# A graph layer on one core: eight of nine one-hot tiles of a part's sums move from VectorE to GpSimd, between the gathers

## The chip, the core and the metric

The kernel runs on one core of one Trainium2 chip. A core has five engines that run side by side and meet at semaphores: TensorE (PE in the profile; PEld is its weight load), VectorE (DVE), ScalarE (ACT), GpSimd (POOL) and SyncE (SP), which only issues DMAs here. The metric is the device time of one execution in microseconds; smaller is better.

## The reference

A graph of 12,500 nodes with 128 features and 412,500 edges, sorted by destination, goes through one gated message-passing layer, a residual and a layer norm:

```python
theta = x[dst] - x[src]
w = sigmoid(relu(theta @ W1 + b1) @ W2 + b2)
agg = segment_sum(w * theta, dst, num_segments=n_nodes)
indeg = segment_sum(ones((E, 1)), dst, num_segments=n_nodes)
y = x + agg + indeg * (x @ W4 + b4)
out = (y - mean(y)) / sqrt(var(y) + 1e-5)        # over the 128 features
```

All of it is float32. The edge list is an input, so what is gathered and summed where is known only at run time.

## The kernel before

**Parts.** The sorted edges are cut into parts, each with a window of at most 112 destination rows. A table `z` in HBM holds `x @ W1` and `x` side by side, so that one gathered row of 256 floats serves the gate and the message. The first 26 parts (`PLAIN`) are handled in a simple way while the table and lookup tiles are being made. The other 234, the *later parts*, are the bulk of the time and the place of the change. Two successive parts make a block with one window.

**A later part.** It has two kinds of source. Eight tiles of 128 edges are gathered from `z`, one indirect DMA of GpSimd each (L380). Their slots come in pairs that share a destination, so four one-hot tiles `ow` (128 edges x 112 window rows) serve all eight. Another five tiles of 128 edges (`HQ`) come from *hot* lookups: ScalarE writes one-hot tiles `of` (L966, L968), TensorE multiplies them with resident tables (L980), ScalarE moves the result to `xT` (L994). They have five one-hot tiles `owh` of their own. The nine tiles `ow` and `owh` are "the one-hot tiles of the sums": TensorE multiplies them with the weighed messages and adds up into the PSUM tile `pa` (L1083, in `add_part`).

**The order of work.** For later parts the instructions of TensorE, VectorE and ScalarE run in the order in which `part(s)` writes them:

- VectorE: `logits` (L896, L898, L899), the five hot logits (L1054), the weighing of four gathered tiles (L928) with a gate that ScalarE makes (L903), then `owh` (L1066) and `ow` (L873). Then comes the end of the block before: in the first part of a pair `finish` (L1129, which waits for ScalarE's `total`, L1121), in the second `normalize` (L1156, L1162 and on). Last come some steps of `place`, which sorts the edges of the next 64 parts (L549, L552, L641 to L643 and others).
- ScalarE: tiles `of`, the gate (L903), hot weights (L1057, L1063), the weighing of the other four tiles (L919), `total` and so on.
- TensorE: `add_part(s - 1)`, hot products, then `products_ahead(s + 1, s + 2)` (L1021, L1025, L1029, L1040).

Both one-hots are written as one comparison each, of a row of column numbers (`iota_f`, a copy in PSUM) with each edge's row in the window (`rel` and `hrel`, bf16, one value to a partition and tile): 4 x 112 and 5 x 112 elements. `ow` has 4 buffers, `owh` 2.

**GpSimd's queue.** It holds gathers and, between every two of them, a filler: a no-operation in the first eight parts, later a memset of 128 x 320 floats that nobody reads (`rest_t`, L374). `part(s)` issues the gathers of part s+3 (`LEAD`). The first of the eight waits for the newest matmul that was issued when it was written (`paced`). There are six tiles `zbuf` for the gathered rows, used in a ring. GpSimd takes its operands from SBUF only; `iota_row` is the SBUF form of the row of column numbers.

Of the kernel before, what the change touches and what calls it, by code (L numbers as in the profile page):

```python
# [9 lines left out]
F32 = mybir.dt.float32  # L10
# [5 lines left out]
OP = mybir.AluOpType  # L16
# [4 lines left out]
P = 128  # L21
D = 128
K = 8
J = K // 2
# [3 lines left out]
WB = 112  # L28
# [10 lines left out]
LEAD = 3  # L39
LB = 5  # L40
NH = 8
# [11 lines left out]
HQ = HK // P  # L53
# [27 lines left out]
def gnn_resnorm(  # L81
# [37 lines left out]
    nc = tc.nc  # L119
# [36 lines left out]
    def set_of(s):  # L156

        s0 = 0 if s < PLAIN else PLAIN + (s - PLAIN) // S2 * S2
        return placed[s0], s - s0
# [42 lines left out]
    def early(n, dtype=F32):  # L202

        a = used_of[0]
        used_of[0] = a + -(-n // (2 if dtype == BF16 else 1))
        assert used_of[0] <= HR * HT * D
        t = tabs_flat[:, a:used_of[0]]
        return t if dtype == F32 else t.bitcast(dtype)
# [37 lines left out]
    iota_row = const.tile([P, P], F32, name="iota_row")  # L246
# [9 lines left out]
    rest = early(D)  # L256
# [7 lines left out]
    for i, t in enumerate(terms):  # L264
        at = slice(i * HALF // 2, i * HALF // 2 + 1)
# [9 lines left out]
    iota_f = fix[:, :WB].rearrange("p (o m) -> p o m", o=1)  # L275
# [60 lines left out]
    def pairs(s):  # L336
        return J if s < NF else JT

    def slots(s):
        return [h * J + j for h in range(2) for j in range(pairs(s))]  # L340
# [11 lines left out]
    def rows_of(s):  # L352
        return own_of(s)[:, :, :D] if s < NH else ring(s)[:, :, :2 * D]
# [11 lines left out]
    rest_t = const.tile([P, 320], F32, name="rest_t")  # L365
    table_steps = []
    paced = {}

    def gather(s):

        (src_i, _, _), i = set_of(s)
        for k in slots(s):
            if gathers:
                rest = nc.gpsimd.memset(rest_t, 0.0) if s >= NH else nc.gpsimd.engine_nop()  # L374
                tc.add_manual_dep(
                    rest.ins, gathers[-1].ins.name,
                    mybir.DependencyInfo(mybir.DependencyClass.NoSync, mybir.DependencyReason.DATA),
                    reason="between two gathers")
                gathers.append(rest)
            ins = nc.gpsimd.indirect_dma_start(  # L380
                out=rows_of(s)[:, k, :], out_offset=None, in_=z if s >= NH else x,
                in_offset=IndirectOffsetOnAxis(ap=src_i[:, k, i:i + 1], axis=0))
            waits = [(gathers[-1], mybir.DependencyClass.NoSync)] if gathers else []
            at = (s * K + k) * 4 * len(chunks) // (NH * K) - 6
            if s < NH and 0 <= at < len(table_steps):
                waits.append((table_steps[at], mybir.DependencyClass.Sync))
            if k == 0 and s in paced:
                waits.append((paced[s], mybir.DependencyClass.Sync))
            for other, kind in waits:
                tc.add_manual_dep(  # L390
                    ins.ins, other.ins.name,
                    mybir.DependencyInfo(kind, mybir.DependencyReason.DATA), reason="gathers' pace")
            gathers.append(ins)


    base_b = const.tile([1, NK], I32, name="base_b")
# [280 lines left out]
    with tc.manual_schedule(engines={SP}), tc.tile_pool(name="work", bufs=2) as wp, tc.tile_pool(  # L677
        name="ps_y", bufs=2, space=bass.MemoryType.PSUM
    ) as ps_y, tc.tile_pool(
        name="ps_l", bufs=1, space=bass.MemoryType.PSUM  # L680
    ) as ps_l:
        parts, blocks = {}, {}
# [18 lines left out]
        def bank(name="pxa"):  # L701
            return ps_l.tile([P, P * G], F32, name=name)
# [77 lines left out]
        def load_u(b):  # L780

            u = blocks[b]["u"] = wp.tile([P, D], F32, name="u", bufs=3)
            nc.sync.dma_start(u[:WB], u_d[ds(blocks[b]["base"], WB), :])
# [62 lines left out]
        def spread_y(s):  # L846
# [17 lines left out]
                                            y_of(s), start=s >= NH, stop=True, skip_group_check=s < NH)  # L864
            return last

        def one_hot_w(s):

            (_, rel, _), i = set_of(s)
            parts[s]["ow"] = []  # L870
            for k0 in range(0, K if s < PLAIN else J, J):
                ow = wp.tile([P, J, WB], F32, name="ow", bufs=4)
                nc.vector.tensor_tensor(  # L873
                    ow, iota_f.to_broadcast([P, J, WB]),
                    rel[:, k0:k0 + J, i:i + 1].to_broadcast([P, J, WB]), op=OP.is_equal)
                parts[s]["ow"].append(ow)
# [24 lines left out]
        def open_gate(s):  # L901

            nc.scalar.activation(gate[:, s % 2], parts[s]["lg"][:, :, 0], AF.Sigmoid, bias=b2_c)  # L903
# [26 lines left out]
        def weigh_rest(s):  # L930
            scale_rows(s, range(KV, K))

        def hot_set(s):

            s0 = PLAIN + (s - PLAIN) // S2 * S2
            return hots[s0], s - s0
# [11 lines left out]
        def hot_load(f):  # L948

            i0, g, i1, i = f  # L950
            a = i0
            while a < i1:
                (hot_s, _, n), j = hot_set(a)
                m = min(i1 - a, n - j)
                nc.sync.dma_start(
                    hot_src[:, i % NU, (a - i0) * EP:(a - i0 + m) * EP],
                    hot_s[g, j:j + m].rearrange("(o p) l e -> o (p l e)", o=1).to_broadcast([P, m * EP]))
                a += m
# [48 lines left out]
        def hot_x(s, q):  # L1007
            return parts[s]["hx"][:, q * P:(q + 1) * P] if q < G else parts[s]["hz"][:, P:2 * P]
# [50 lines left out]
        def hot_weights(s):  # L1059

            wx = parts[s]["wxh"]
            for q in range(HQ):
                nc.scalar.activation(wx[:, q, :D], hot_x(s, q), AF.Copy, scale=wx[:, q, D:D + 1])  # L1063
            (_, hrel, _), j = hot_set(s)
            owh = parts[s]["owh"] = wp.tile([P, HQ, WB], F32, name="owh")
            nc.vector.tensor_tensor(  # L1066
                owh, iota_f.to_broadcast([P, HQ, WB]),
                hrel[:, j, :].rearrange("p (q o) -> p q o", o=1).to_broadcast([P, HQ, WB]), op=OP.is_equal)

        def shift(b):  # L1070

# [51 lines left out]
        def finish(b):  # L1123

            d = blocks[b]
            a = d["a"]
            plain = b * SUB < PLAIN
            if not plain:
                nc.vector.tensor_add(a[:WB], a[:WB], d["pa"][:, 0, :])  # L1129
# [55 lines left out]
        def fetch(b):  # L1185
            if b < NK:
                load_block(b)
# [66 lines left out]
        def due_at(s, lead):  # L1254
            return [f for f in rest_of if f[0] - lead == s]
# [87 lines left out]
        def part(s):  # L1343

            b, h = divmod(s, SUB)
            credit[0] = min(credit[0] + (2.15 if s < PLAIN + S2 else 1.9), 6.0)
            if s in turns:
                edges[s + 3] = turns[s], load(turns[s])
            if s in edges:
                i, loaded = edges.pop(s)  # L1350
                assert steps[0] is None
                steps[:] = place(i, lambda: bank("last"), *loaded), "k"
            for f in rest_of:
                if f[0] - 5 == s:
                    hot_load(f)
            if h == 0:
                fetch(b + 2)
                if b - 1 in blocks and "u" not in blocks[b - 1]:
                    load_u(b - 1)
            ended = PLAIN // SUB <= b - 1 < NK  # L1360
            if opened:
                hot_out(*opened.pop())
            now = due_at(s, 3)
            if now:
                hot_tiles(now[0])
            if h == 1 and s + 3 < NS:
                one_hot(s + 3)
            if s < NS:
                logits(s)
            if PLAIN + AHEAD <= s + LEAD < NS:  # L1370
                if s >= PLAIN + 4:
                    paced[s + LEAD] = newest[0]
                gather(s + LEAD)
            if PLAIN <= s - 1 < NS:
                add_part(s - 1)
            if now:
                opened.append((now[0], hot_products(now[0])))
            if s < NS:
                open_gate(s)
                hot_logits(s)  # L1380
                weigh(s)
                hot_weights(s)
                gate_sums(s)
                one_hot_w(s)
                if now[1:]:
                    hot_out(*opened.pop())
                    hot_tiles(now[1])
                weigh_rest(s)
                advance("p")
                products_ahead(s + 1, s + 2)  # L1390
                if now[1:]:
                    opened.append((now[1], hot_products(now[1])))
            if h == 0 and ended:
                total(b - 1)
                finish(b - 1)
                own(b - 1)
            if h == 1:
                if s < NS:
                    shift(b)
                if ended:  # L1400
                    normalize(b - 1)
            spend("ksnmz")
# [7 lines left out]
    with tc.tile_pool(name="post_ps", bufs=1, space=bass.MemoryType.PSUM) as pps:  # L1410
        one = const.tile([P, 1], F32, name="one")
# [195 lines left out]
```

## Time and profile before

| | |
|---|---|
| Times of three runs | 3405.97, 3414.64, 3415.90 us (median 3414.64) |
| The profiled execution | 3395.38 us, span 3393.6 us |
| Granted TensorE clock, mean | 0.885 |
| Busy: PE, PEld | 2713.4, 2351.2 us |
| Busy: DVE, ACT, POOL | 2641.6, 2363.5, 2821.6 us |
| Later parts, in time | from about 413 us to the end |

Lines of the profile name the engine, the source line, the operation, output<-inputs and a count; "idle before" is the time that the engine stood still just ahead of the instruction, and after the arrow stands what ended it. "issue" means that nothing the profile shows was being waited for; "remote" is a source that the profile can't name. The engines' busy times overlap, so none of them is the time of the kernel, and the end of a matmul is modelled.

### The profile page before, as it was taken

The numbers are of one execution on the slowest core, as the hardware profiler recorded it, in microseconds if no ns is written. First come the engines' busy times: TensorE is split into PE (matmuls) and PEld (weight loads), VectorE is DVE, ScalarE is ACT, GpSimd is POOL, SyncE is SP. The second block draws the span as 40 slices with busy tenths as digits, with TensorE's granted clock in tenths as the row PEclk, the third lists the DMA queues.
The fourth block names the chain that finished last, engine by engine and source line by source line (L and its number), as shares of the span: only waits on it lengthen the run. The fifth ranks groups of instructions, "written<-read, shape, count | busy, mean of one in ns | idle before, by whom it ended". The sixth has DMA issues, their size and how long they took to land.

```text
span 3393.6 us, 62355 instructions
## 1 busy us (share of the span) xinstructions
PE 2713.4 (80%) x18615; PEld 2351.2 (69%) x18615; DVE 2641.6 (78%) x6197; ACT 2363.5 (70%) x5856; POOL 2821.6 (83%) x4093
## 2 busy tenths in 40 slices
PE   6776778787788787888788878888878888888887
PEld 5676767676677676777677766676667777677776
DVE  6797458898888689888888858888887866666666
ACT  4554567776677677777777767777767777777774
POOL 5678778888888888888888888888888888888883
PEclk9876678898899888999898889899988999998998
DMA  7564434444444444444444444444444444444441
GB/s 255 184 169 121 119 93 121 118 111 117 121 113 120 128 113 116 121 117 121 122 118 120 116 118 123 117 117 124 116 115 123 115 122 117 119 122 118 126 110 55
DMA packets 265060, 416.67 MB, mean 123 GB/s; under 512 B 66608, under 2 KB 178217, under 8 KB 264205
## 3 DMA queue, kind: packets, MB, share of 16 engines
q0 software_dynamic: 98528, 267.78, 28.5%
q1 hardware_dynamic: 164219, 138.42, 15.6%
q10 hardware_dynamic: 1970, 6.40, 0.5%
q8 instruction: 154, 2.52, 0.3%
q14 instruction: 189, 1.55, 0.2%
HBM read 384.89 MB, written 27.49 MB: 122 GB/s over the span
## 4 chain that ended last, share of the span: by engine, by line
DVE 30%; ACT 25%; PE 16%; issue 11%; POOL 8%; DMA 5%; another core or an unknown queue 4%; DVEq 0%; SPq 0%; POOLq 0%; ACTq 0%
POOL zbuf L380 6%; ACT wxh L1063 5%; PE pd L980 4%; DVE hh L1054 4%; DVE zbuf L896 4%; DVE zbuf L898 4%; ACT zbuf L919 4%; DVE lg L899 4%; ACT of L966 4%; PE pa L1083 4%; POOL rest_t L374 2%; DMA zbuf<-z,src_i 2%; ACT of L968 2%; DVE ed L549 2%
## 5 line engine op out<-in xcount | busy, mean ns | idle before, releaser
L380 POOL DMA_INDIRECT zbuf<-z,src_i x1866 | 1816.1, 973 | 421.0 <-issue 261.6
L980 PE MATMUL pd<-of,tabs 128*128 128x128 f32 (+4 forms) x4816 | 685.9, 298 | 181.6 <-ACT of L968 95.8
L374 POOL MEMSET rest_t<- 128x320 f32 x2010 | 800.4, 398 | 1.0
L980 PEld LDWEIGHTS pd<-of,tabs 128*128 128x128 f32 x4816 | 628.9, 209 | 224.7 <-ACT of L968 113.5
L1083 PE MATMUL pa<-zbuf,ow 128*112 128x260 f32 (+1 forms) x2282 | 588.1, 406 | 47.6 <-ACT zbuf L919 21.6
L1083 PEld LDWEIGHTS pa<-zbuf,ow 128*112 128x112 f32 x2282 | 407.4, 200 | 157.7 <-ACT zbuf L919 30.1
L1025 PE MATMUL pxa<-wni,xT 128*128 128x128 f32 x1872 | 303.8, 311 | 258.0 <-DVE hh L1054 241.5
L1025 PEld LDWEIGHTS pxa<-wni,xT 128*128 128x128 f32 x1872 | 266.1, 218 | 281.8 <-DVE hh L1054 261.0
L966 ACT ACTIVATE of<-hot_src,nodes 128x512 f32<-128x512 f16 (+3 forms) x602 | 394.1, 709 | 7.1 <-issue 4.3
L919 ACT ACTIVATE zbuf<-zbuf 128x128 f32<-128x128 f32 x1144 | 362.8, 389 | 0.4
L1040 PE MATMUL y<-y,oh 64*128 64x128 f32 x1872 | 341.1, 323 | 14.2 <-issue 14.0
L1029 PE MATMUL pxa<-y,oh 64*128 64x128 f32 x1872 | 336.9, 323 | 9.9 <-issue 9.6
L1054 DVE SCALAR_TENSOR_TENSOR hh<-pxa,w_r 128x128 f32<-128x128 f32 x936 | 270.7, 289 | 92.9 <-remote 48.2
L1083 PEld LDWEIGHTS pa<-wxh,owh 128*112 128x112 f32 x2340 | 295.2, 177 | 34.8 <-issue 12.6
L968 ACT ACTIVATE of<-of 128x1024 f32<-128x1024 f32 (+3 forms) x301 | 310.8, 1033 | 9.2
L1083 PE MATMUL pa<-wxh,owh 128*112 128x130 f32 x2340 | 308.9, 276 | 5.8 <-issue 4.4
L994 ACT ACTIVATE xT<-pd 128x512 f32<-128x512 f32 (+7 forms) x496 | 185.7, 416 | 183.2 <-PE pd L980 59.5
L1029 PEld LDWEIGHTS pxa<-y,oh 64*128 64x128 f32 x1872 | 275.2, 219 | 49.5 <-issue 26.9
L928 DVE TENSOR_TENSOR zbuf<-zbuf,fix 128x512 f32<-128x512 f32 x234 | 160.2, 684 | 186.4 <-ACT fix L903 118.9
L896 DVE TENSOR_TENSOR zbuf<-y,zbuf 128x1024 f32<-128x1024 f32 x234 | 285.5, 1220 | 13.5 <-issue 3.5
L898 DVE SCALAR_TENSOR_TENSOR zbuf<-zbuf,fix 128x1024 f32<-128x1024 f32 x234 | 285.7, 1221 | 8.0
L899 DVE TENSOR_REDUCE lg<-zbuf 128x8 f32<-128x1024 f32 x234 | 285.5, 1220 | 8.0
(265 smaller groups left out, 4710.0 us busy)
## 6 DMA issues: line engine op xcount, KB each, us to landing
to_all<-off_d SPq DMA_DIRECT2D x234, 144.0 KB
hot_src<-hot_s SPq DMA_DIRECT2D x257, 128.0 KB
zbuf<-z,src_i POOLq DMA_INDIRECT x1866
z<-zbuf SPq DMA_DIRECT2D x8, 1024.0 KB
xw<-in_x_dram SPq DMA_DIRECT2D x130, 56.0 KB
u<-u_d SPq DMA_DIRECT2D x130, 56.0 KB
out_dram<-o SPq DMA_DIRECT2D x130, 56.0 KB
y<-z SPq DMA_DIRECT2D x252, 28.0 KB
```

The lines of the kernel that those rows point to most:

```text
L374: rest = nc.gpsimd.memset(rest_t, 0.0) if s >= NH else nc.gpsimd.engine_nop()
L380: ins = nc.gpsimd.indirect_dma_start(out=rows_of(s)[:, k, :], out_offset=None, in_=z if s >= NH else x, in_offset=IndirectOffsetOnAxis(ap= ...
L896: nc.vector.tensor_sub(half, yy.to_broadcast([P, 2, J, D]), half)
L898: nc.vector.scalar_tensor_tensor(h, h, 0.0, w2.to_broadcast([P, K, D]), op0=OP.max, op1=OP.mult)
L899: nc.vector.tensor_reduce(lg[:, :, 0], h, AX.X, OP.add)
L919: nc.scalar.activation(wx[:, k, :D], wx[:, k, :D], AF.Copy, scale=wx[:, k, D:D + 1])
L966: nc.scalar.activation(of[:, t, :], hot_src[:, i % NU, :w], AF.Abs, bias=nodes[:, t:t + 1])
L980: newest[0] = nc.tensor.matmul(to[:, q], tabs[:, g * RG + q, t, :], of[:, t, q], start=t == 0, stop=t == HT - 1)
L1025: nc.tensor.matmul(hot_y(s, q), xT[:, q * P:(q + 1) * P], wneg, start=q % G == 0, stop=False, skip_group_check=True)
L1029: newest[0] = nc.tensor.matmul(hot_y(s, q), d["oh"][:, BP + q * P:BP + (q + 1) * P], y_of(s), start=False, stop=True, skip_group_check=True)
L1054: nc.vector.scalar_tensor_tensor(h, hot_y(s, q), 0.0, w2_r, op0=OP.max, op1=OP.mult, accum_out=lg[:, q, :])
L1083: newest[0] = nc.tensor.matmul(to if len(w.shape) == 3 else to[:, 0, :], one, w, start=first and i == 0, stop=last and i == len(terms) - 1)
```

## The change

GpSimd makes the four tiles `ow` and four of the five tiles `owh` of part s+1, each with a `tensor_scalar` of 128 x 112 elements (`iota_row` compared with the edge's row), while it issues the gathers of part s+3: one ahead of each gather, where the memset stood. VectorE's L873 falls away for these parts, and L1066 makes only the last tile of `owh`. `owh` has three buffers instead of two. The first two and the last two of the later parts are made by VectorE as before. The last batch has only two gathers; the six one-hots left over follow it.

```diff
-    def gather(s):
+    def gather(s, between=()):
 
         (src_i, _, _), i = set_of(s)
+        between = list(between)
         for k in slots(s):
             if gathers:
-                rest = nc.gpsimd.memset(rest_t, 0.0) if s >= NH else nc.gpsimd.engine_nop()
+                if between:
+                    rest = between.pop(0)()
+                else:
+                    rest = nc.gpsimd.memset(rest_t, 0.0) if s >= NH else nc.gpsimd.engine_nop()
                 tc.add_manual_dep(
...
             gathers.append(ins)
+        for fill in between:
+            fill()
...
+        made = {}
+
+        def one_hots_between(s):
+
+            (_, rel, _), i = set_of(s)
+            (_, hrel, _), j = hot_set(s)
+            ow = wp.tile([P, J, WB], F32, name="ow", bufs=4)
+            owh = wp.tile([P, HQ, WB], F32, name="owh", bufs=3)
+            made[s] = ow, owh
+            iota = iota_row[:, :WB]
+
+            def one(to, at):
+                return lambda: nc.gpsimd.tensor_scalar(to, iota, at, None, op0=OP.is_equal)
+
+            return ([one(ow[:, k, :], rel[:, k, i:i + 1]) for k in range(J)]
+                    + [one(owh[:, q, :], hrel[:, j, q:q + 1]) for q in range(K - J)])
+
         def one_hot_w(s):
 
             (_, rel, _), i = set_of(s)
+            if s in made:
+                parts[s]["ow"] = [made[s][0]]
+                return
...
-            owh = parts[s]["owh"] = wp.tile([P, HQ, WB], F32, name="owh")
+            owh, q0 = (made[s][1], K - J) if s in made else (wp.tile([P, HQ, WB], F32, name="owh", bufs=3), 0)
+            parts[s]["owh"] = owh
             nc.vector.tensor_tensor(
-                owh, iota_f.to_broadcast([P, HQ, WB]),
-                hrel[:, j, :].rearrange("p (q o) -> p q o", o=1).to_broadcast([P, HQ, WB]), op=OP.is_equal)
+                owh[:, q0:, :], iota_f.to_broadcast([P, HQ - q0, WB]),
+                hrel[:, j, q0:].rearrange("p (q o) -> p q o", o=1).to_broadcast([P, HQ - q0, WB]),
+                op=OP.is_equal)
...
-                gather(s + LEAD)
+                gather(s + LEAD, one_hots_between(s + 1))
```

## The prediction

> **What bounds the kernel now.** I read the page first, then busy time by stretches of 500 us, then the groups of VectorE by shape, then the order of time of GpSimd.
>
> ```profile
> span 3393.6 us, 62355 instructions
> PE 2713.4 (80%) x18615; PEld 2351.2 (69%) x18615; DVE 2641.6 (78%) x6197; ACT 2363.5 (70%) x5856; POOL 2821.6 (83%) x4093
> DVE 30%; ACT 25%; PE 16%; issue 11%; POOL 8%; DMA 5%; another core or an unknown queue 4%; DVEq 0%; SPq 0%; POOLq 0%; ACTq 0%
> L380 POOL DMA_INDIRECT zbuf<-z,src_i x1866 | 1816.1, 973 | 421.0 <-issue 261.6
> L374 POOL MEMSET rest_t<- 128x320 f32 x2010 | 800.4, 398 | 1.0
> ```
>
> No engine is full, and the chain that ended last changes between VectorE, ScalarE and TensorE: a loop of short waits. GpSimd has the largest busy share and only two kinds of work, gather and memset. The order of time shows its idle time in detail (start, duration, idle before):
>
> ```profile
> 1830.30 0.95 POOL L380 DMA_INDIRECT zbuf<-z,src_i  x1 [0.17 <-issue]
> 1831.25 0.38 POOL L374 MEMSET rest_t<- 128x320 f32 x1
> 1831.80 0.95 POOL L380 DMA_INDIRECT zbuf<-z,src_i  x1 [0.17 <-issue]
> 5.63 0.94 POOL L380 DMA_INDIRECT zbuf<-in_x_dram,src  x1 [0.30 <-issue]
> 6.88 0.94 POOL L380 DMA_INDIRECT zbuf<-in_x_dram,src  x1 [0.30 <-issue]
> ```
>
> A slot of one gather and one memset is 1.50 us from start to start: 0.95 + 0.38 + 0.17 of issue. The 0.17 is not free time. With a no-operation in the memset's place (the last two rows) a slot is 1.25 us, so the memset costs 0.25 us of spacing, not its 0.38.
>
> ```profile
> 1000.00:1500.00 500.00, 405.57 (x2847) 352.96 (x2848) 412.35 (x946) 366.84 (x909) 436.88 (x632) 0.90 0.45 120
> 1500.00:2000.00 500.00, 408.13 (x2871) 351.96 (x2870) 405.14 (x959) 367.19 (x915) 438.43 (x638) 0.90 0.45 121
> 2000.00:2500.00 500.00, 407.80 (x2891) 352.33 (x2890) 435.40 (x995) 370.59 (x917) 437.85 (x637) 0.92 0.45 119
> 2500.00:3000.00 500.00, 410.27 (x2868) 351.55 (x2868) 352.98 (x870) 365.00 (x909) 429.38 (x632) 0.91 0.43 118
> ```
>
> The columns are PE, PEld, DVE, ACT and POOL, busy us with instructions in brackets. A later part has 16 GpSimd instructions, so these 2000 us hold 2539 / 16 = 158.7 parts of 12.60 us. GpSimd was busy 1742.5 us in them; with 0.17 us for each of 1269.5 gathers (215.8 us) its own need is 1958.3 / 158.7 = 12.34 us a part. **It has 0.26 us of slack in 12.60, or 33 ns in each of eight slots.** That is the tightest resource here; the rest is the loop of waits.
>
> **The change part by part.** It covers 230 of the 234 later parts.
>
> *Removed from VectorE.* These are its groups by shape:
>
> ```profile
> L873 DVE TENSOR_TENSOR ow<-fix,rel 128x448 f32<-128x448 f32 x286 | 175.4, 614 | 34.6 <-PE pa L1083 17.9 <-remote 16.7
> L1066 DVE TENSOR_TENSOR owh<-fix,hrel 128x560 f32<-128x560 f32 x234 | 171.7, 734 | 0.0
> L928 DVE TENSOR_TENSOR zbuf<-zbuf,fix 128x512 f32<-128x512 f32 x234 | 160.2, 684 | 186.4 <-ACT fix L903 118.9 <-issue 31.4 <-ACT oh L839 30.8
> L1129 DVE TENSOR_TENSOR a<-a,pa 112x130 f32<-112x130 f32 x117 | 34.1, 291 | 200.1 <-ACT a L1121 121.3 <-ACT zbuf L919 52.2 <-issue 24.4
> L1054 DVE SCALAR_TENSOR_TENSOR hh<-pxa,w_r 128x128 f32<-128x128 f32 x936 | 270.7, 289 | 92.9 <-remote 48.2 <-PE pd L980 12.3 <-PE pa L1083 5.3
> L1054 DVE SCALAR_TENSOR_TENSOR hh<-last,w_r 128x128 f32<-128x128 f32 x234 | 68.2, 292 | 62.8 <-remote 37.1 <-PE pa L1083 2.7 <-PE pd L980 2.2
> L1162 DVE SCALAR_TENSOR_TENSOR v<-u,sw,own_f 112x128 f32<-112x128 f32 x117 | 41.7, 356 | 5.7 <-DMA u<-u_d 1.5
> L1156 DVE TENSOR_TENSOR own_f<-own_f,a 112x128 f32<-112x128 f32 x130 | 36.1, 277 | 15.7 <-ACT own_f L1138 10.4 <-ACT oh L827 5.1 <-issue 0.2
> ```
>
> L873 goes whole: 0.614 us. L1066 keeps one tile of five. Between 448 and 560 elements the time grows by 120 ns, 1.07 ns an element, so 112 elements are about 0.25 us (estimate) and 0.48 us goes. That is 1.09 us a part, 252 us of busy time. Most of it is not on the path. In the first part of each pair the next thing VectorE does after these two is L1129, and it already waits there 200.1 / 117 = 1.71 us for ScalarE's total: 1.09 us less ahead of it makes that wait 1.09 us longer, worth nothing. In the second part of a pair (115 of them) no such wait follows and the next part's L896 starts earlier: at most 115 x 1.09 = 126 us. But the next waits are L928 for the gate and L1054 for the products, 186.4 + 92.9 + 62.8 = 342 us or 1.46 us a part, and where one stands already it only grows. It stands in some parts and not in others; I take half: **-63 us**, with 0 and -126 as the ends.
>
> *Added to GpSimd.* Eight compares of 112 columns for eight memsets of 320. The trace has no such compare. Nearest are GpSimd's small operations at the start:
>
> ```profile
> 0.99 0.23 POOL L247 IOTA iota_row<- 128x128 f32 x1
> 1.19 0.28 POOL masks.py:199 TENSOR_SCALAR_AFFINE_SELECT wni<-wni 128x128 f32<-128x128 f32 x1
> 1.44 0.13 POOL L250 IOTA iota_p<- 128x1 f32 x1
> 1.53 0.23 POOL L253 IOTA lag<- 128x128 f32 x1
> ```
>
> The affine select reads and writes 128 columns and compares, in 0.28 us; at about 1 ns a column (the memset's 0.38 against these) 112 columns are 0.26. It lacks the per-partition value that the compare fetches. Lower end: no cost for that, 0.26 + 0.17 issue = 0.43 against the memset's 0.55, a slot shorter by 0.12 us. Upper end: the fetch costs a whole one-column operation (0.13), and the gap before the next gather is 0.30 as behind a no-operation: 0.28 + 0.13 + 0.30 = 0.71, longer by 0.16. I take the affine select and 0.09 for the fetch, the spacing of the one-column IOTA (1.44 to 1.53): 0.26 + 0.09 + 0.17 = 0.52, **shorter by 0.03 us a slot**, since that row is nearest in kind. GpSimd then needs 12.1 us a part and stays off the path: 0 us. The affine select is one instruction, and the price hangs on it.
>
> The GPSIMD Engine Reference of the Trainium skill (§ 3.1) speaks against the change: about 2.6 cycles an element for two inputs, though § 4.1 calls one-input work roughly line-rate. An estimate by the first is 112 x 2.6 / 1.2 GHz = 243 ns of streaming, by the second 93 ns; the affine select's row sits nearer to the second.
>
> *Contention.* The compare reads SBUF, the memset did not. What sharing does is seen here:
>
> ```profile
> 1827.22 0.95 POOL L374 MEMSET rest_t<- 128x320 f32 x1
> 1828.34 1.42 POOL L380 DMA_INDIRECT zbuf<-z,src_i  x1 [0.16 <-issue]
> 1827.29 0.59 DVE L641 TENSOR_SCALAR ed<-ew 128x829 int32<-128x829 int32 x1
> 1827.91 1.02 DVE L642 SCALAR_TENSOR_TENSOR et<-ed,ew 128x829 int32<-128x829 int32 x1
> ```
>
> A memset beside L641 took 0.95 instead of 0.38 us, a gather beside L642 (two SBUF inputs) 1.42 instead of 0.95. So L1156 and L1162, also with two SBUF inputs, can now meet a compare: 234 or so of them, a compare open in 8 x 0.26 / 12.60 = 17% of the time, half of 0.26 us each: 5 us, and as much again for operations like L642: **+10 us** (ends 0 and 60, if nearly each one waited a whole compare). The skill's SBUF — State Buffer page (§ Who interferes with whom) has the rule: an instruction with two SBUF inputs contends with a GpSimd instruction that reads SBUF, not with one that only writes. The gather's row agrees.
>
> *The new wait.* The one-hots for part s+1 ride between the gathers for part s+3, so TensorE's sums now wait for GpSimd two parts earlier than VectorE does for that batch.
>
> ```profile
> 3022.03 0.95 POOL L380 DMA_INDIRECT zbuf<-z,src_i  x1 [0.95 <-PE pd L980]
> 3032.51 0.95 POOL L380 DMA_INDIRECT zbuf<-z,src_i  x1 [0.17 <-DVE lg L899]
> 3039.50 2.01 PE L1083 MATMUL pa<-zbuf,ow 128*112 128x260 f32 x8
> 0.00:1960.00 1960.00, 1169.34 (x1190) 0.87 0.47 128
> 0.00:2100.00 2100.00, 1255.14 (x1278) 0.87 0.47 128
> 0.00:1960.00 1960.00, 147.52 (x121) 0.87 0.47 128
> 0.00:2100.00 2100.00, 159.71 (x131) 0.87 0.47 128
> ```
>
> The batch from 3022.03 to 3032.51 would carry the one-hots of the sums at 3039.50: 7 us to spare. The last four rows count gathers (208 belong to early parts) and L896. At 2100 us GpSimd was in batch 134 and VectorE in part 131; at 1960 in 123 and 121, one part less ahead. That is 12.6 us, more than the 7, so a wait of up to about 5 us there. Behind a GpSimd wait all later gathers queue, but its own new waits, for free buffers, are on sums of part s-2 or earlier, and the first gather of the batch is already held for a later matmul: nothing. I price the late one-hots at **+5 us**.
>
> Sum: -63 + 10 + 5 + 0 = **-48 us**, on 3395.4 us (span 3393.6 and 1.8 around it): 3347. The median of the runs, 3414.6, lies 0.6% above that execution; on its scale **3366**.
>
> **The rivals.**
> *GpSimd becomes the bound (slower).* A slot longer by more than 33 ns uses up the slack, and from there each further 10 ns costs 230 x 8 x 10 ns = 18 us, whatever VectorE gains. At +0.10 us, between that point and the upper end, GpSimd needs 13.14 us a part: 230 x 0.54 = +124, 3539; at +0.16, 13.62 and +235, 3650. For it: 33 ns is less than the uncertainty of my one row. Against it: that row. The 2.6 cycles above would put the kernel here.
> *VectorE's relief is worth nothing (same).* From 2000–2500 to 2500–3000 VectorE's busy time fell by 82 us and the parts did not come faster (637 and 632 instructions). If the loop through ScalarE and GpSimd sets the pace, 3415. Against it: stretches of 500 us average over quite different waits.
>
> **How the numbers follow.** What a measurement can tell here is 0.3%, 10 us. Forecast 0.48, GpSimd bound 0.41, no difference 0.11; so faster 0.48, same 0.11, slower 0.41. Low: the full 126 us less 15 and some 5 of spread: 3300 to 3310, I take 3310. High: to hold eight in ten it must reach into the rival, past its middle: 3550. Its faster case alone would be 3310 to 3400.
>
> **What would show it.** Right: gather to gather under 1.50 us with a compare between; GpSimd's need under 12.4 us a part; L873 at 56 instructions and L1066 at about 0.25 us; L1129's idle time up by about 1 us each; gathers still held by TensorE at batch starts. Wrong: slots over 1.53 us, no idle time before batches, and TensorE's L1083 or VectorE's L896 waiting for GpSimd or a gather's DMA: then the rival holds.

## The result, and the profile after

The changed kernel takes 3900.9 us (median of four runs) where the kernel before takes 3410.3: **1.144 times as long** (95% interval 1.1407 to 1.1468). The forecast was 3366 us and the range ended at 3550. The profiled execution took 3903.1 us.

The page's first part and the chain of the changed kernel:

```profile
span 3901.4 us, 62806 instructions
PE 2924.9 (75%) x18615; PEld 2530.1 (65%) x18615; DVE 2416.6 (62%) x5967; ACT 2382.6 (61%) x5856; POOL 3353.8 (86%) x4099
POOL 35%; PE 19%; ACT 17%; DVE 11%; issue 11%; DMA 6%; SPq 1%; another core or an unknown queue 0%; POOLq 0%; DVEq 0%; ACTq 0%
```

VectorE did lose 225 us of work (2641.6 to 2416.6), almost the predicted 252. But GpSimd gained 532 us, and its share of the chain went from 8% to 35%. The groups by shape (busy time, mean ns | idle time before) name the work:

```profile
L384 POOL DMA_INDIRECT zbuf<-z,src_i x1866 | 1949.0, 1044 | 348.8 <-issue 262.2 <-ACT of L994 27.5 <-DMA zbuf<-z,src_i 9.8
L885 POOL TENSOR_SCALAR ow<-iota_row,rel 128x112 f32<-128x112 f32 x920 | 565.6, 615 | 32.0
L885 POOL TENSOR_SCALAR owh<-iota_row,hrel 128x112 f32<-128x112 f32 x920 | 559.7, 608 | 31.6
L1111 PE MATMUL pa<-wxh,owh 128*112 128x130 f32 x2340 | 541.1, 346 | 775.4 <-POOL owh L885 773.9
L922 DVE TENSOR_TENSOR zbuf<-y,zbuf 128x1024 f32<-128x1024 f32 x234 | 286.0, 1222 | 371.3 <-DMA zbuf<-z,src_i 359.9 <-issue 6.1 <-remote 3.3
L1093 DVE TENSOR_TENSOR owh<-fix,hrel 128x112 f32<-128x112 f32 x230 | 61.6, 268 | 0.0
L1157 DVE TENSOR_TENSOR a<-a,pa 112x130 f32<-112x130 f32 x117 | 34.1, 291 | 513.6 <-ACT a L1149 328.3 <-issue 147.7 <-ACT zbuf L945 37.6
```

L384 is the gather (L380 before), L885 the new compare, L1111 the sums (L1083), L922 VectorE's first step on gathered rows (L896), L1093 and L1157 the former L1066 and L1129. A compare is busy for 0.61 us; the prediction had 0.35. TensorE waits 774 us for the `owh` that GpSimd makes, VectorE 360 us for gathered rows. The order of time on GpSimd (start, duration, idle before):

```profile
2000.18 0.58 POOL L885 TENSOR_SCALAR ow<-iota_row,rel 128x112 f32<-128x112 f32 x1
2000.93 1.03 POOL L384 DMA_INDIRECT zbuf<-z,src_i  x1 [0.17 <-issue]
2002.00 0.59 POOL L885 TENSOR_SCALAR ow<-iota_row,rel 128x112 f32<-128x112 f32 x1
2002.76 1.03 POOL L384 DMA_INDIRECT zbuf<-z,src_i  x1 [0.17 <-issue]
```

Gather to gather is 1.83 us (2000.93 to 2002.76): 1.03 of gather, 0.04 to the compare, 0.59 of compare, 0.17 of issue. It was 1.50. Busy time by stretches of 500 us (PE, PEld, DVE, ACT, POOL, then clock, DMA share, GB/s):

```profile
1000.00:1500.00 500.00, 376.37 (x2401) 324.27 (x2399) 311.38 (x796) 315.93 (x777) 445.30 (x531) 0.84 0.38 101
1500.00:2000.00 500.00, 378.87 (x2403) 326.88 (x2404) 329.96 (x814) 310.92 (x766) 444.78 (x537) 0.85 0.38 100
2000.00:2500.00 500.00, 373.07 (x2418) 318.93 (x2418) 303.93 (x748) 312.77 (x768) 444.86 (x535) 0.85 0.37 100
2500.00:3000.00 500.00, 379.91 (x2442) 327.54 (x2442) 324.47 (x814) 312.74 (x773) 444.47 (x539) 0.85 0.38 101
3000.00:3500.00 500.00, 374.34 (x2414) 320.26 (x2410) 253.50 (x649) 314.45 (x774) 444.48 (x539) 0.86 0.37 101
```

GpSimd's 2681 instructions in 2500 us are 167.6 parts of 14.92 us. Eight slots of 1.83 and the 0.34 us that the prediction counted beside the slots (12.34 - 8 x 1.50) make 14.98. So GpSimd now sets the pace, with no idle time beyond the issue between its instructions. The 2.32 us that each of 230 parts became longer make 534 us; the span grew by 507.8.

### The profile page after: what moved, and what is told of

Read it like the earlier page. It is cut to its first block, busy times and chain, and to the rows that moved or that the text cites. A ratio compares the mean times of both kernels' runs of the same rounds, so it can differ in the third digit from the quotient of the medians.

```text
span 3901.4 us, 62806 instructions
## 1 busy us (share of the span) xinstructions
PE 2924.9 (75%) x18615; PEld 2530.1 (65%) x18615; DVE 2416.6 (62%) x5967; ACT 2382.6 (61%) x5856; POOL 3353.8 (86%) x4099
## 4 chain that ended last, share of the span: by engine, by line
POOL 35%; PE 19%; ACT 17%; DVE 11%; issue 11%; DMA 6%; SPq 1%; another core or an unknown queue 0%; POOLq 0%; DVEq 0%; ACTq 0%
POOL zbuf L384 22%; POOL owh L885 8%; PE pd L1006 7%; POOL ow L885 5%; DMA zbuf<-z,src_i 4%; PE pa L1111 4%; ACT wxh L1089 3%; ACT of L992 3%; DVE hh L1080 2%; ACT zbuf L945 2%; DVE zbuf L924 2%; DVE zbuf L922 2%; DVE lg L925 2%; ACT oh L844 1%; ACT of L994 1%
## 5 line engine op out<-in xcount | busy, mean ns | idle before, releaser
L384 POOL DMA_INDIRECT zbuf<-z,src_i x1866 | 1949.0, 1044 | 348.8 <-issue 262.2
L1111 PE MATMUL pa<-wxh,owh 128*112 128x130 f32 x2340 | 541.1, 346 | 775.4 <-POOL owh L885 773.9
L1111 PEld LDWEIGHTS pa<-wxh,owh 128*112 128x112 f32 x2340 | 374.5, 208 | 946.6 <-POOL owh L885 931.4
L1006 PE MATMUL pd<-of,tabs 128*128 128x128 f32 (+4 forms) x4816 | 855.1, 352 | 37.0 <-ACT of L994 26.1
L1006 PEld LDWEIGHTS pd<-of,tabs 128*128 128x128 f32 x4816 | 825.9, 266 | 48.7 <-ACT of L994 28.3
L885 POOL TENSOR_SCALAR ow<-iota_row,rel 128x112 f32<-128x112 f32 x920 | 565.6, 615 | 32.0
L1111 PE MATMUL pa<-zbuf,ow 128*112 128x260 f32 (+1 forms) x2282 | 552.9, 388 | 51.2 <-ACT zbuf L945 28.9
L885 POOL TENSOR_SCALAR owh<-iota_row,hrel 128x112 f32<-128x112 f32 x920 | 559.7, 608 | 31.6
L922 DVE TENSOR_TENSOR zbuf<-y,zbuf 128x1024 f32<-128x1024 f32 x234 | 286.0, 1222 | 371.3 <-DMA zbuf<-z,src_i 359.9
L1111 PEld LDWEIGHTS pa<-zbuf,ow 128*112 128x112 f32 x2282 | 381.4, 189 | 148.7 <-ACT zbuf L945 31.1
L1157 DVE TENSOR_TENSOR a<-a,pa 112x130 f32<-112x130 f32 x117 | 34.1, 291 | 513.6 <-ACT a L1149 328.3
L1055 PE MATMUL pxa<-y,oh 64*128 64x128 f32 x1872 | 275.4, 288 | 0.0
```

The lines of the kernel that those rows point to most:

```text
L384: ins = nc.gpsimd.indirect_dma_start(out=rows_of(s)[:, k, :], out_offset=None, in_=z if s >= NH else x, in_offset=IndirectOffsetOnAxis(ap= ...
L885: return lambda: nc.gpsimd.tensor_scalar(to, iota, at, None, op0=OP.is_equal)
L922: nc.vector.tensor_sub(half, yy.to_broadcast([P, 2, J, D]), half)
L1006: newest[0] = nc.tensor.matmul(to[:, q], tabs[:, g * RG + q, t, :], of[:, t, q], start=t == 0, stop=t == HT - 1)
L1111: newest[0] = nc.tensor.matmul(to if len(w.shape) == 3 else to[:, 0, :], one, w, start=first and i == 0, stop=last and i == len(terms) - 1)
```

## Experiments

The runs came in five groups, each with its own runs of the kernel before, and that kernel did not take the same time in each: 3306 us (two groups, e1 to e4 and e5 to e8), 3406 (e9 to e12), 3350 (e13 to e16), 3363 (e17 and e18). The record's 3410 is like the third. Every ratio below is to the kernel before in its own group, with a 95% interval. The record gives each group a chip number (7, 0, 4, 0 and 3), and number 0 stands for e5 to e8, where the kernel before took 3306 us, and for e13 to e16, where it took 3350. So the number alone does not decide it; whether the groups differ by the chip or by its condition at the time is not known.

**Is it the slot alone?** e1 leaves the kernel before as it is and only makes the memset longer; VectorE keeps all its work. e5 is the changed kernel in a group of 3306.

```diff
-    rest_t = const.tile([P, 320], F32, name="rest_t")
+    rest_t = const.tile([P, 696], F32, name="rest_t")
...
-                rest = nc.gpsimd.memset(rest_t, 0.0) if s >= NH else nc.gpsimd.engine_nop()
+                rest = (nc.gpsimd.memset(rest_t if s >= PLAIN + AHEAD else rest_t[:, :320], 0.0)
+                        if s >= NH else nc.gpsimd.engine_nop())
```

> The kernel before, with the memset between the gathers of the later parts lengthened from 320 to 696 columns, so that a slot lasts about 1.83 us (0.95 + 0.71 + 0.17) as in the changed kernel; VectorE makes all one-hots, nothing new waits for GpSimd. Theory 'queue' (the loss is GpSimd's own time, eight slots a part): 230 x 8 x 0.33 us more need less the 0.26 us of slack a part, 3880 to 3960 us. Rival 'lateness' (part of the loss comes from TensorE waiting for one-hots two parts ahead of their batch): clearly less than the changed kernel, under 3800 us. Rival 'contention' (GpSimd's SBUF reads stop VectorE): under 3800 us too, since a memset reads nothing.

> The changed kernel itself, on the same chip as the next three, so that they can be compared. Queue theory: slots of 1.83 us, and the time that the long memset's run gave for slots of 1.81 us (3833) plus 230 x 8 x 0.02 us: about 3870 on that chip, the ratio to the kernel before 1.14 to 1.18.

e1: 3833.4 us, 1.159 (1.1575 to 1.1613). e5: 3870.8 us, 1.170 (1.1678 to 1.1719). e1's order of time on GpSimd, and its group of VectorE's first step:

```profile
2003.49 0.95 POOL L381 DMA_INDIRECT zbuf<-z,src_i  x1 [0.17 <-issue]
2004.43 0.70 POOL L374 MEMSET rest_t<- 128x696 f32 x1
2005.30 0.95 POOL L381 DMA_INDIRECT zbuf<-z,src_i  x1 [0.17 <-issue]
L897 DVE TENSOR_TENSOR zbuf<-y,zbuf 128x1024 f32<-128x1024 f32 x234 | 286.4, 1224 | 633.9 <-DMA zbuf<-z,src_i 632.8 <-issue 0.3 <-PE y L1041 0.2
```

A slot of 1.81 us (2003.49 to 2005.30) gives nearly the whole loss with no one-hot moved. The difference from e5's slot of 1.83 is 0.02 us in rows that are rounded to 0.01; times 1840 slots that is some 37 us, and 37.4 were measured. With that rounding the agreement is good to about 20 us. So the rest of the change, taken together, is worth little beside the slot.

**What makes the compare dear?** e3 takes away the per-partition value; e4 puts rows of GpSimd operations behind the last gather of the kernel before, in one profiled run (3335 us, in a group of 3306).

```diff
-                return lambda: nc.gpsimd.tensor_scalar(to, iota, at, None, op0=OP.is_equal)
+                return lambda: nc.gpsimd.tensor_scalar(to, iota, 5.0, None, op0=OP.is_equal)
```

> The changed kernel, with the edge's row replaced by the constant 5.0 in GpSimd's compares, so no per-partition value is fetched (the one-hots hold other values). If the fetch of that value is what makes the compare 0.59 us instead of 0.35: 0.35 to 0.45 us, slots of 1.6 to 1.7 us, 3550 to 3700 us. If the cost is in the elements or in the compare itself: still 0.55 to 0.59 us and 3850 to 3910 us.

> The kernel before, with GpSimd operations written to a spare tile behind the last gather, four of each in a row: memset of 112 and 320 columns, compares with a constant, an f32 and a bf16 per-partition value at 28 to 448 columns, an addition of a constant, a two-input subtraction, a copy and an affine select. Queue theory: the bf16 compare of 112 columns is about 0.5 to 0.6 us from start to start. By the widths: if it is the elements, 448 columns take nearly four times as long; if it is a fixed cost (fetching the value, dispatch), 28 columns take over 0.4 us. Time of the kernel about 3420 us, the added work standing behind the gathers.

e3: 3930.4 us, 1.189 (1.1862 to 1.191), slower than the change and not faster. Its order of time:

```profile
1999.49 1.03 POOL L384 DMA_INDIRECT zbuf<-z,src_i  x1 [0.27 <-issue]
2000.59 0.50 POOL L885 TENSOR_SCALAR owh<-iota_row 128x112 f32<-128x112 f32 x1
2001.35 1.03 POOL L384 DMA_INDIRECT zbuf<-z,src_i  x1 [0.27 <-issue]
```

The compare is 0.09 us shorter, but the gap behind it is 0.10 longer (0.27) and the one ahead of it 0.03, and the slot is 1.86 us (1999.49 to 2001.35). So the fetch of the value takes 0.09 of the 0.59 us, which is what the prediction gave it; the other 0.50 is where the price lies. e4's operations, grouped by shape:

```profile
L1417 POOL TENSOR_SCALAR oh<-tabs,iota_p 128x448 f32<-128x448 f32 x4 | 5.5, 1400 | 0.0
L1418 POOL TENSOR_SCALAR oh<-tabs,col_b 128x112 f32<-128x112 f32 x4 | 2.2, 560 | 0.0
L1416 POOL TENSOR_SCALAR oh<-tabs 128x112 f32<-128x112 f32 x4 | 1.9, 486 | 0.3
L1419 POOL TENSOR_SCALAR oh<-tabs 128x112 f32<-128x112 f32 x4 | 2.0, 492 | 0.3
L1420 POOL TENSOR_TENSOR oh<-tabs 128x112 f32<-128x112 f32 x4 | 1.6, 419 | 0.1
L1421 POOL COPY oh<-tabs 128x448 f32<-128x448 f32 x4 | 2.1, 555 | 0.0
L1421 POOL COPY oh<-tabs 128x112 f32<-128x112 f32 x4 | 0.9, 273 | 0.0
L1422 POOL TENSOR_SCALAR_AFFINE_SELECT oh<-tabs 128x112 f32<-128x112 f32 x4 | 1.0, 270 | 0.0
L1415 POOL MEMSET oh<- 128x112 f32 x4 | 0.7, 196 | 10.8 <-PE pxa L1029 10.8
```

L1417 and L1418 are the compare with an f32 and a bf16 value (each 560 ns at 112 columns and 1400 at 448), L1416 the compare with a constant; L1419 adds a constant. At 112 columns the affine select takes 270 ns and the compare 560, twice that. From 112 to 448 columns the compare grows by 840 ns, 2.5 ns a column; the copy by 282, 0.84 ns a column. The addition is as dear as the compare with a constant (492 ns against 486), and the affine select, which compares too, is not. So it is the kind of instruction and not the comparison.

**Do the one-hots come late?** e9 is the changed kernel with them made one part earlier.

```diff
-            owh = wp.tile([P, HQ, WB], F32, name="owh", bufs=3)
+            owh = wp.tile([P, HQ, WB], F32, name="owh", bufs=4)
...
-                gather(s + LEAD, one_hots_between(s + 1))
+                gather(s + LEAD, one_hots_between(s + 2))
```

> The changed kernel with the one-hots made a whole part earlier: between the gathers for part s+3 stand those of part s+2 instead of s+1 (owh with four buffers). Queue theory: TensorE's long wait for GpSimd's owh (774 us in the changed kernel's trace) is GpSimd's slowness seen from TensorE, so the ratio stays at 1.16 to 1.18. Lateness theory: with a part more of lead that wait goes and the ratio falls under 1.12.

e9: 3906.0 us, 1.1455 (1.1436 to 1.1474). Its groups of the sums and of VectorE's first step:

```profile
L1111 PE MATMUL pa<-wxh,owh 128*112 128x130 f32 x2340 | 302.8, 275 | 9.9 <-POOL owh L885 9.8
L922 DVE TENSOR_TENSOR zbuf<-y,zbuf 128x1024 f32<-128x1024 f32 x234 | 286.4, 1224 | 875.7 <-DMA zbuf<-z,src_i 863.0 <-issue 9.0 <-remote 3.1
```

The largest wait of the changed kernel is gone (774 to 10 us), and the time is the same: VectorE now waits 863 us for gathered rows instead of 360. The 774 us were a symptom. Whoever depends on GpSimd waits, and the wait shows wherever it ends last.

**What is VectorE's relief worth?** e2 and e16 (the same kernel in another group) keep the memset between the gathers (`return ()` hands over nothing to put there) and leave the eight one-hots out on both engines; the sums read a tile of zeros, `still`, in their place. That changes what TensorE multiplies too, and the two effects are not separated.

```diff
+        still = const.tile([P, J, WB], F32, name="still")
+        nc.vector.memset(still, 0.0)
...
-            made[s] = ow, owh
+            made[s] = still, owh
+
+            return ()
```

> VectorE's relief alone: the memset of 320 columns stays between the gathers, VectorE makes only the ninth one-hot, and the eight others are left out (the sums read one fixed tile of zeros in their place). GpSimd's slot stays at 1.50 us. The prediction's term: -63 us, with 0 and -126 as its ends, so 3285 to 3410, likeliest 3350. Rival (GpSimd or the loop through ScalarE sets the pace already): no change, 3400 to 3415.

> VectorE's relief alone once more, with the memset between the gathers as in before (eight of nine one-hot tiles left out, a tile of zeros read instead). It ran at 0.996 where before took 3306 us. Theory 'GpSimd sets the pace in before': 0.99 to 1.00 on either chip. Theory 'on the slower chip VectorE sets more of the pace, as the prediction had it': 0.96 to 0.985 where before takes about 3406 us.

e2: 0.996 (0.9946 to 0.9975), 12 us of 3306. e16: 0.9936 (0.9914 to 0.9958), 20 us of 3350. In e2 GpSimd holds the rest back, by the groups of gather and VectorE's first step:

```profile
L384 POOL DMA_INDIRECT zbuf<-z,src_i x1866 | 1815.9, 973 | 327.1 <-issue 259.2 <-ACT zbuf L941 14.5 <-ACT of L988 6.7
L918 DVE TENSOR_TENSOR zbuf<-y,zbuf 128x1024 f32<-128x1024 f32 x234 | 285.7, 1221 | 253.8 <-DMA zbuf<-z,src_i 249.6 <-issue 1.4
```

VectorE waits 250 us for gathers, and 259 of the 327 us of GpSimd's idle time ahead of them are issue (in the kernel before 262 of 421): little slack is left to it.

**Would the assumed price have met the forecast?** e6, e15 and e18 are one kernel, in three groups: everything of the change, with a copy of 112 columns for each compare, so that the one-hot tiles hold column numbers. Its slot is near the assumed 1.47 us.

```diff
-                return lambda: nc.gpsimd.tensor_scalar(to, iota, at, None, op0=OP.is_equal)
+                return lambda: nc.gpsimd.tensor_copy(to, iota)
```

> The changed kernel with each of GpSimd's compares replaced by a copy of the same 112 columns of the row of column numbers (0.22 us from start to start in a row, against 0.54 for the compare; the one-hots hold column numbers). All else of the change stays: the reads of SBUF, the buffers, TensorE's wait for GpSimd two parts ahead, VectorE's relief. If the compare's price is the only step that failed: slots of 1.45 to 1.50 us and a ratio of 0.98 to 1.00. If lateness or contention cost something by themselves: a ratio over 1.01 in spite of slots under 1.5 us.

> The change with a copy of 112 columns in place of each compare once more: the price that the prediction assumed (a slot of about 1.43 us). The one-hots then hold column numbers, so the sums are left wrong. It ran at 0.966 where before took 3306 us. Theory 'the price of the compare alone spoiled the forecast': 0.96 to 0.99 also where before takes about 3406 us (the forecast was 0.986). Theory 'a shorter slot costs time on that chip whatever fills it': 1.03 to 1.17 there.

> The change with the copy of 112 columns for the compare a third time: the price that the prediction assumed. The one-hots hold column numbers, so the sums are left wrong. 0.966 where before took 3306 us, 1.004 where it took 3350. Theory 'the chip decides': on the same line, 1.03 to 1.06 if before takes about 3406 us in this run; 0.96 to 0.97 if 3306; 1.00 if 3350. Theory 'the price alone spoiled the forecast': 0.97 to 1.00 at 3406 too.

e6: 0.966 (0.9643 to 0.9675). e15: 1.004 (1.0015 to 1.0064). e18: 1.004 (1.0017 to 1.0063). e6's order of time:

```profile
1999.38 0.97 POOL L384 DMA_INDIRECT zbuf<-z,src_i  x1 [0.17 <-issue]
2000.36 0.28 POOL L885 COPY owh<-iota_row 128x112 f32<-128x112 f32 x1
2000.81 0.97 POOL L384 DMA_INDIRECT zbuf<-z,src_i  x1 [0.17 <-ACT zbuf L945]
```

With a slot of 1.43 us the loss of 14 to 17% is gone, so the buffers, the new wait and VectorE's shorter step do no harm of that size. But the gain of 3.4% is there in one group only. Where the kernel before takes 3350 or 3363 us the same kernel is 0.4% slower, outside the forecast of 0.986. What it would give in a group of 3406 was not run.

**Fewer one-hots.** e8 and e17 (one kernel) move three of the hot one-hots and put no-operations in the other five slots, for a mean slot of 1.47 us; e11 moves one.

```diff
-            return ([one(ow[:, k, :], rel[:, k, i:i + 1]) for k in range(J)]
-                    + [one(owh[:, q, :], hrel[:, j, q:q + 1]) for q in range(K - J)])
+            a, b, c = (one(owh[:, q, :], hrel[:, j, q:q + 1]) for q in range(3))
+            none = nc.gpsimd.engine_nop
+            return [none, a, none, none, b, none, none, c]
```

> GpSimd makes three one-hot tiles of owh in three of the eight slots and a no-operation stands in the other five; VectorE makes ow whole and two tiles of owh. GpSimd needs 3 x 1.83 + 5 x 1.25 = 11.74 us a part against 11.96 before, and VectorE is relieved of 0.36 us. Queue theory: a ratio of 0.97 to 0.995, faster than both kernels if no rest is needed. Rival (any compare on GpSimd costs by lateness or contention): over 1.00.

> Three of the hot one-hots on GpSimd with the compare, no-operations in the other five slots, once more: a mean slot of (3 x 1.83 + 5 x 1.25) / 8 = 1.47 us, just under the 1.50 of before. It ran at 0.979 where before took 3306 us. Theory 'the mean slot sets the time everywhere': 0.975 to 1.00 on any chip. Theory 'a shorter slot costs time on the slower chips': between the one compare's 1.090 at a mean slot of 1.32 us and 1 at 1.50, so about 1.015 where before takes 3350 us or more.

> GpSimd makes one tile of owh in one of the eight slots and a no-operation stands in the other seven; VectorE makes the other eight tiles. GpSimd needs 1.83 + 7 x 1.25 = 10.58 us a part (10.0 without the compare, 11.74 with three). Queue theory: between the run without rest (0.958) and the one with three (0.979): 0.955 to 0.965. If the relief of 0.12 us is worth more than the 0.58 us of GpSimd: under 0.955.

e8: 0.979 (0.9771 to 0.9816). e17: 1.000 (0.9986 to 1.0016). e11: 1.090 (1.0886 to 1.0923), in the group of 3406. e8 beats the kernels before and after in its group, and nothing is left of that in e17's. e11, whose mean slot is 1.32 us, is far slower than before: there a shorter slot costs time.

**No rest at all.** e7 and e13 (one kernel) put a no-operation for the memset in the kernel before (from the fifth later part on), e12 and e14 (one kernel) nothing at all, e10 the no-operation and VectorE's relief. The slot is 1.25 us in each.

```diff
-                rest = nc.gpsimd.memset(rest_t, 0.0) if s >= NH else nc.gpsimd.engine_nop()
+                rest = (nc.gpsimd.memset(rest_t, 0.0) if NH <= s < PLAIN + AHEAD
+                        else nc.gpsimd.engine_nop())
```

> The kernel before, with a no-operation in place of the memset between the gathers of the later parts from the fifth on: slots of 1.25 us, nothing else changed. Queue theory, with GpSimd's slack already used up on this chip: faster, a ratio of 0.97 to 0.99, the rest set by VectorE and ScalarE. Rival (the memset's rest keeps gathers from crowding something): 1.00 or slower.

> The kernel with a no-operation for the memset once more. It ran at 0.958 of the time of before where before took 3306 us; three relatives with the same short slot ran at 1.09 to 1.17 where before took 3406 us. Theory 'the chip decides': at 0.95 to 0.97 if before takes about 3306 us in this run, at 1.05 to 1.20 if it takes about 3406. Theory 'the kernel decides': 0.95 to 0.97 on either.

> The kernel before with nothing at all between the gathers of the later parts from the fifth on. GpSimd already waits for TensorE at many batch starts without the rest, so a still shorter slot should bring little: 0.95 to 0.96, against 0.958 with no-operations. If gathers back to back hold each other up: slots over 1.25 us and a ratio over 0.965.

> The kernel with nothing at all between the gathers once more (1.158 where before took 3406 us). Its gather to gather is 1.25 us, as with the no-operation. Theory 'the chip decides': at the same side of 1 as the no-operation in this run, 0.95 to 0.97 if before takes about 3306 us, 1.1 to 1.2 if about 3406. Theory 'the kernel decides': 1.1 to 1.2 on either, with the no-operation at 0.96 beside it.

> VectorE's relief alone as in the run before (the eight one-hots left out, a fixed tile of zeros read in their place), but with a no-operation in place of the memset, so GpSimd is not the bound. If the relief was worth only 0.4% there because GpSimd held the pace: now a good deal more over the run without rest (0.958), by the prediction's term of 63 us about 0.94. If VectorE's one-hots are hidden behind ScalarE's waits whatever GpSimd does: 0.955 to 0.96.

| Mean slot, us | Kernel | before at 3306 | at 3350, 3363 | at 3406 |
|---|---|---|---|---|
| 1.25 | no-operation | 0.958 (e7) | 1.162 (e13) | |
| 1.25 | nothing between | | 1.135 (e14) | 1.158 (e12) |
| 1.25 | no-operation, relief | | | 1.172 (e10) |
| 1.32 | one one-hot | | | 1.090 (e11) |
| 1.43 | copy, relief | 0.966 (e6) | 1.004 (e15, e18) | |
| 1.47 | three one-hots | 0.979 (e8) | 1.000 (e17) | |
| 1.50 | memset, relief | 0.996 (e2) | 0.994 (e16) | |
| 1.81 | longer memset | 1.159 (e1) | | |
| 1.83 | the change | 1.170 (e5) | | 1.144 (record) |
| 1.83 | the change, one-hots earlier | | | 1.146 (e9) |
| 1.86 | the change, constant | 1.189 (e3) | | |

The intervals of e7, e13, e12, e14 and e10 are 0.9565 to 0.9597, 1.1593 to 1.1652, 1.155 to 1.1611, 1.1301 to 1.1407 and 1.169 to 1.1747. The mean slots of e8, e17 and e11 are worked out from slots of 1.83 and 1.25. At 3306 the time falls with the slot all the way. Elsewhere it is lowest near the slot that the kernel before has. The expectations of e10, e11 and e12 were built on e7's 0.958, and all three missed. e7 and e13 are the same program, 3178 and 3892 us long. TensorE's waits (total, times, longest) in e13, then in e7:

```profile
PE y L1041 <- issue: 161.9, 211, 1.8
PE pxb L1022 <- issue: 147.7, 189, 1.8
PE pxa L1030 <- issue: 106.9, 146, 1.9
PE last L1026 <- issue: 50.1, 70, 1.2
```

```profile
PE pxa L792 <- issue: 5.6, 1, 5.6
PE y L864 <- issue: 3.7, 2, 2.2
PE last L729 <- issue: 0.2, 1, 0.2
```

The four lines are e13's largest of this kind; in e7 the three lines are all that there is of it. In e13 TensorE stands still again and again with nothing to wait for that the profile shows. GpSimd has time to spare in e13 and waits for TensorE, which now leads the chain (the largest of GpSimd's waits, the largest wait of all, then the chain by engine):

```profile
POOL zbuf L381 <- PE last L1030: 646.7, 165, 14.4
ACT xT L995 <- remote: 726.2, 169, 7.0
PE 45%; ACT 19%; issue 13%; another core or an unknown queue 11%; DVE 8%; DMA 2%; SPq 1%; POOL 0%; DVEq 0%; POOLq 0%; ACTq 0%
```

The order of time on TensorE in e13 shows the size of such pauses, and the cores' line of each run the mean clock:

```profile
2014.37 0.50 PE L1030 MATMUL pxa<-y,oh 64*128 64x128 f32 x2
2015.32 0.36 PE L1041 MATMUL y<-y,oh 64*128 64x128 f32 x1 [0.45 <-issue]
2016.73 0.27 PE L1041 MATMUL y<-y,oh 64*128 64x128 f32 x1 [1.05 <-issue]
core 0: 3892.0 us, clock 0.810
```

```profile
core 0: 3178.3 us, clock 0.900
```

So two things grow where a short rest costs time: pauses of 0.45 and 1.05 us in TensorE, and the time at the lower clock. That GpSimd is not the brake there is shown, and TensorE leads the chain. What makes it pause is not shown: 11% of the chain and the largest wait, ScalarE's at L995, are for a source that the profile can't name.

The pauses are not new in e13. The kernel before has them in the record's trace; the largest of their lines there is this one:

```profile
PE pd L980 <- issue: 82.7, 108, 4.7
```

All such lines of a trace, added up, come to 193 us in 322 pauses for the kernel before and to 585 us in 753 for e13. None of e1 to e8, the groups of 3306, has more than 21 us, whatever its slot. In the other groups it goes by the mean slot: 34 and 36 us at 1.83 (e9 and the changed kernel), 97 to 230 at 1.43 to 1.50 (e15 to e18 and the kernel before), 466 to 652 at 1.25 to 1.32 (e10 to e14). So the groups differ by whether TensorE pauses, and where it does, a shorter slot goes with more time in pauses. The changed kernel, which GpSimd holds back, has few of them, and it took nearly the same time in both kinds of group (3871 and 3901 us).

## Why the prediction was wrong, point by point

- **GpSimd as the tightest resource, 33 ns a slot of slack: right for a longer slot.** So was the rule of the first rival, 18 us for each 10 ns beyond it. The slot grew by 0.33 us; 230 x 8 x (0.33 - 0.033) = 546 us, and the span grew by 508. For a shorter slot the prediction had 0 us; e7 shows a gain of 4% in its group and e13 a loss of 16% in another.
- **The price of the compare: wrong, and the step that failed.** The forecast took 0.35 us from the affine select; in its slot the compare takes 0.59. With 0.08 us more for the gather behind it and 0.04 ahead of it the slot is 1.83 instead of 1.47. Of the two parts of the 0.35, the 0.09 for the fetch held (e3: 0.59 with it, 0.50 without); the 0.26 for the rest was 0.50. The upper bound failed as well: +0.16 us, against +0.33. It was built from the same kind of row, with the fetch and the gap behind it as the only unknowns; e3 and e4 show that the kind of instruction has a price of its own.
- **The rule that spoke against the change was nearer.** By e4 the streaming of 112 columns costs 112 x 2.5 = 280 ns, and as much again does not depend on the width. The GPSIMD Engine Reference of the Trainium skill (§ 3.1) gave an estimate of 243 ns for streaming at two inputs; the line-rate for one input (§ 4.1) holds here for the copy (0.84 ns a column) and not for the compare. The prediction set the affine select's row, 0.28 us at 128 columns, nearer to the lower of the two estimates; as it stands, 0.28 is nearer to the higher one.
- **VectorE's relief, -63 us: wrong in size.** e2 and e16 give -12 and -20. Half of the parts that could gain was a choice between 0 and -126, made without the prediction's own first finding: at an unchanged slot GpSimd allows 0.26 us a part, 230 x 0.26 = 60 us at the very most. The second rival, that the relief is worth nothing, was nearer on this term. Both runs are of groups in which the kernel before was faster than in the record; at 3406 the relief with the memset was not run.
- **Late one-hots, +5: no cost was found.** The wait came, 774 us of it, but as the sign of a slow GpSimd: e9 takes it away and the time stays. e6 has the same order with a cheaper operation and gains in its group all the same.
- **Contention, +10: about right on VectorE's side, not separated on GpSimd's.** In the changed kernel's trace L1156's operation (L1184 there) takes 298 ns on average instead of 277, L1162's (L1190) 377 instead of 356, and L642's (L648) 16 to 23 more: 6 us of busy time in all. The compare's mean in the kernel is 0.61 us, and 0.56 in a row behind the last gather in e4; 1840 x 0.05 = 92 us is what sharing could have cost the compares, more than the 60 allowed.
- **The sum with the right price for the wrong operation.** Even a slot of 1.43 us gave 0.966 in one group and 1.004 in two. The forecast, 0.986, lies between and describes neither. That a shorter slot could itself cost time, where TensorE pauses, was in no rival.
- **What would show it:** slots over 1.53 us, no idle time before batches, and L1083 and L896 waiting for GpSimd and for gathers. All three are there.

## What to carry to other kernels

Before moving work into an engine's gaps, measure the exact instruction there, at its size and in its slot: two operations that look alike on paper can differ by a factor of two, and a repeated slot multiplies the error (here by 1840). Give the relieved engine no more credit than the slack of the next one. When one engine sets the pace, the largest wait in the profile only says who noticed, and taking that wait away moves it.

## What the runs showed of the hardware

- On GpSimd a compare with a per-partition value takes 560 ns at 112 columns and grows by 2.5 ns a column up to 448. At 112 columns a compare with a constant takes 486, an addition of a constant 492, a subtraction of two inputs 419, a copy 273, an affine select 270, a memset 196 (all e4).
- What stands ahead of a gather changes its length: 1.03 us behind a compare and 0.97 behind a copy (e3, e6), which read, and 0.95 behind a memset or a no-operation (e1, e13), which do not.
- The same program can differ by 22% between groups of runs (e7 and e13), and the sign of an edit with it. Where TensorE pauses with nothing to wait for that the profile shows, taking out a filler that nobody reads made the kernel 14 to 16% slower (e13, e14, e12).
- In e7, by the order of time on TensorE, eight matmuls take 1.16 us behind 1.39 us of idle time and 2.08 us behind 4.44. The granted clock is 1.00 during the first and 0.50 during the second:

```profile
2003.11 1.16 PE L1026 MATMUL pxa<-wni,xT 128*128 128x128 f32 x8 [1.39 <-DVE hh L1055]
2016.68 2.08 PE L1026 MATMUL pxa<-wni,xT 128*128 128x128 f32 x8 [4.44 <-DVE hh L1055]
```

The Trainium skill's page TensorE: Matmul & The Clock Gate (section HAM oscillation) has this as a rule: idle gaps of more than about 3.4 us let the clock fall to half. These two rows agree. Most falls of the clock have no such gap ahead of them, though. Between 450 and 3000 us, by the clock records of the traces, the clock falls to half 84 times in e7 and 161 times in e13, and TensorE has 29 and 11 idle gaps over 3.4 us; in the changed kernel it is 135 falls and 4 gaps. So the rule alone does not account for the low mean clock of e13, nor for its pauses.
